# Reciprocals of the WKV recurrence in two steps of 256 columns

## The chip, the cores and the metric

The kernel runs on one core of a Trainium2 chip. The core has a matrix engine (PE), three engines for elementwise work (DVE, ACT and POOL) and SP, whose queue issues most of the transfers. Each engine takes its instructions in the order of its own queue, and semaphores hold an instruction back until what it needs is there. The metric is the device time of one execution in microseconds (us), less being better. Before the change the median of three runs is 1221.08 us (1217.28 to 1223.45).

## The reference, cut to what matters

The input x has 16 sequences of 512 tokens with 256 channels. It is normalised to `xn`; one branch is an RWKV layer (time mixing with a recurrence, then channel mixing), the other a mixture of eight experts that picks tokens by rank. The result is `x + s * silu(g)`.

```
x = _ln(x, ln0_w, ln0_b);  h = _ln(x, ln1_w, ln1_b);  xx = _time_shift(h)
xk = h * tmk + xx * (1 - tmk)          # likewise xv, xr
k = xk @ Wk.T;  v = xv @ Wv.T;  sr = sigmoid(xr @ Wr.T)
...
def step(carry, kv_t):                 # over the 512 tokens
    ww = u + kt;  p = max(pp, ww);  e1 = exp(pp - p);  e2 = exp(ww - p)
    y = (e1 * aa + e2 * vt) / (e1 * bb + e2)
...
x = x + (sr * att) @ Wo.T;  h2 = _ln(x, ln2_w, ln2_b)
kf = square(relu(xk2 @ Wfk.T));  kv = kf @ Wfv.T
s = x + sigmoid(xr2 @ Wfr.T) * kv
...
probs = softmax(xn @ Wg);  _, top_idx = top_k(probs.T, cap)   # capacity per expert
out = sum over experts e of gate_e * gelu(xn @ W1[e]) @ W2[e]
```

The division in `y` and the sigmoid of `sr` are done together: the kernel multiplies the denominator by `1 + exp(-r)` and takes one reciprocal of the product. That reciprocal is what the change touches.

## The kernel before, in words

A sequence (an "image" b, 0 to 15) is worked on with channels on the 128 partitions and the 512 tokens along the free dimension, in two halves h of 128 channels. `recurrent(b)` (L652) is a generator of nine steps for one image:

- the first normalisation `n_1` and its transposes `nps_1`, from which ACT makes `hp` (L542);
- the mixes `mix_k`, `mix_v`, `mix_r` (L549 on ACT, then L550 on DVE) and the projections k, v, r (PE, L600), copied out by ACT as `kT` (L675), `vT` (L679) and `erT` (L685);
- `wkv` for h = 0 and h = 1 (L606 to L638): a running maximum (scan L619), exponents on ACT (L625 to L628, tile `ex`), two scans (L629, L633), products (L630, L634, L636), the reciprocal (L637) and the product that puts the result back into `vT` (L638);
- the output projection `o` (PE, L643) and its addition to `x0` on DVE (L695); the second normalisation `n_2` (statistics on DVE L229 and L231, the power on POOL, the scaling on ACT L239);
- the transposes `nps_2` and the mixes `mix_k2`, `mix_r2` (L563 on ACT, then L566 on DVE, both reading `nps_2` in PSUM);
- the wide projection `f` (PE, L600, eight blocks), relu and square on ACT (L707, L708) to `kf`;
- `fr` and `kv` (PE, L643), joined on DVE by L733 and L735.

Here `ex_7_0` means the tile `ex` of image 7, half 0, and so on.

Beside it run, in steps dealt out by the list at L903 and the table `rest_of` at L928: the router's logits for all images, then `route()` (L295), a long chain of small steps that finds each expert's threshold bit by bit. One bit is a `Sign` with a sum on ACT (L343), a small matmul `total` on PE (L346) and `took` (L348) and `less` (L354) on DVE. After the bits come the selection and places (L363 to L408 and on to L503), which give the row numbers `holds` and `goes`. From then on `expert(i)` (L742) gathers 256 rows `xs` (POOL, L751), transposes them (`xsps`, PE L757; `xsT`, ACT L759), multiplies by `w1` (`h`, L768), takes the gelu (L773), multiplies by `w2` (`y`, L643), copies the result to `ys` (L780, by whichever engine the framework chooses, DVE or ACT) and scatters it (POOL, L782). Thirty-six expert blocks are always done and a few more if a count says so (L804).

After the experts, `outputs` (L872) and `soon` (L863) read back the expert results `y` (L816, L821) and the stored `s` (L878): ACT takes a tanh (L830), DVE makes the gates (L831) and products (L842), and POOL adds them to the output in DRAM (L845). The last two images are finished directly; the last one loads x again as `xl` (L867, issued at L215) and writes four pieces from SP (L855).

What sets the order: the framework records the instructions, and when the program is built it orders every engine's queue by readiness and by its own estimates of how long instructions take. Where `tc.issue_after` stands, an order is forced. Buffers are taken in rotation: the PSUM pool `pp_tr` (transposes) has two, `pp_mm` (k, v, r, f, h) three, `pp_ot` (o, fr, kv, y) two; in SBUF the tag `eact` has four (the expert activations, later the halves `y9_0`, `y14_0`, `y15_0` and so on).

Of the kernel before, what the change touches and what calls it, by code (L numbers as in the profile page):

```python
# [19 lines left out]
P = 128  # L20
# [6 lines left out]
def rwkv_times_moe_kernel(ctx: ExitStack, tc: tile.TileContext, a, out: bass.AP):  # L27
# [10 lines left out]
    nc = tc.nc  # L38
    x = a["x"]
    B, T, C = x.shape  # L40
# [104 lines left out]
    def col(name, h, of=cols):  # L145
        i = VECS.index(name) * NC + h
        return of[:, i : i + 1]
# [434 lines left out]
    def in_turn(buffers):  # L582
        buffers.append(buffers.pop(0))
        return buffers[-1]
# [21 lines left out]
    def wkv(kT, vT, erT, h, name):  # L606

        k, v, er = kT[:, h, :], vT[:, h, :], erT[:, h, :]
        w, u = wcol[:, h : h + 1], col("time_first", h)
        pp, ba = in_turn(pps), in_turn(bas)
        pp0, ba0 = pp[:, 0:T], ba[:, :, 0:T]
        nc.vector.tensor_tensor_scan(pp[:, 1:], w.to_broadcast([P, T]), k, -1e38, ALU.add, ALU.max)  # L619


        ex = work.tile([P, 5, T], F32, tag="ex", bufs=2, name=f"ex_{name}")
        nc.vector.scalar_tensor_tensor(ex[:, 3, :], pp0, w, k, ALU.add, ALU.subtract)
        nc.vector.scalar_tensor_tensor(ex[:, 4, :], k, u, pp0, ALU.add, ALU.subtract)
        nc.scalar.activation(ex[:, 0, :], ex[:, 3, :], AF.Relu)  # L625
        nc.scalar.activation(ex[:, 2, :], ex[:, 3, :], AF.Relu, scale=-1.0)
        nc.scalar.activation(ex[:, 1, :], ex[:, 4, :], AF.Relu, scale=-1.0, bias=top)
        nc.scalar.activation(ex[:, 0:3, :], ex[:, 0:3, :], AF.Exp, scale=-1.0)  # L628
        nc.vector.tensor_tensor_scan(ba[:, 0, 1:], ex[:, 2, :], ex[:, 0, :], 0.0, ALU.mult, ALU.add)  # L629
        nc.vector.tensor_tensor(  # L630
            ex[:, 3:5, :], ex[:, 0:2, :], v[:, None, :].to_broadcast([P, 2, T]), ALU.mult
        )
        nc.vector.tensor_tensor_scan(ba[:, 1, 1:], ex[:, 2, :], ex[:, 3, :], 0.0, ALU.mult, ALU.add)  # L633
        nc.vector.scalar_tensor_tensor(ba0, ba0, math.exp(-TOP), ex[:, 1:5:3, :], ALU.mult, ALU.add)  # L634
        den = ex[:, 0, :]
        nc.vector.scalar_tensor_tensor(den, er, 1.0, ba0[:, 0, :], ALU.add, ALU.mult)  # L636
        nc.vector.reciprocal(den, den)  # L637
        nc.vector.tensor_tensor(v, ba0[:, 1, :], den, ALU.mult)  # L638

    def token_major(lhsT_of, w, n, j, ps, jj):  # L640
# [11 lines left out]
    def recurrent(b, done, soon):  # L652
# [34 lines left out]
        for h in range(NC):  # L687
            wkv(kT, vT, erT, h, f"{b}_{h}")
            yield
# [299 lines left out]
```

## Time and profile before

| what | value |
|---|---|
| median of 3 runs | 1221.08 us |
| profiled execution | 1215.99 us, its span 1214.2 us |
| PE busy | 1118.9 us (92% of the span) |
| DVE busy | 782.9 us (64%) |
| ACT busy | 714.6 us (59%) |
| POOL busy | 370.6 us (31%) |
| mean granted PE clock | 0.971 |

The profiled execution is 5.1 us shorter than the median; 1.8 us of it lie outside the span. All places in time below are us from the start of the span. A line of a timeline gives the start, the length, the engine, the line of the kernel, the operation, the tiles as out<-in, the shape and the number of instructions merged into the line; behind it, in brackets, the idle time of the engine just before and what ended it. A line of a table of groups gives the group, its busy time in us with the mean of one instruction in ns, and then the engine's idle time before such instructions. PE executes one float32 matmul of the program as two, so its counts are twice the program's.

### The profile page before, as it was taken

The page shows a single profiled execution, that of the slowest core. Times are in us where ns is not written, and L with a number is a line of the kernel's source. Part 1 is how long each engine was busy: PE and PEld are TensorE (multiplying, and loading weights), DVE is VectorE, ACT ScalarE, POOL GpSimd, SP SyncE. Part 2 cuts the span into 40 slices and gives each one's busy share as a digit, 9 for nine tenths or more (in the row PEclk, how much of TensorE's full clock was granted, in tenths as well). Part 3 has the DMA queues.
Part 4 walks back from the last instruction along what each step waited for, and adds up shares of the span by engine and source line. Part 5 has one row for each costly group of instructions (what it writes and reads, how often), then busy time and mean ns, then how long its engine had stood idle before and what let it go on. Part 6 is the DMA issues. An engine that isn't in the chain of part 4 may idle for free. (4 is left out here: it accounts for less than half of the span.)

```text
span 1214.2 us, 12759 instructions
## 1 busy us (share of the span) xinstructions
PE 1118.9 (92%) x4333; PEld 770.6 (63%) x4333; DVE 782.9 (64%) x1324; ACT 714.6 (59%) x1158; POOL 370.6 (31%) x479
## 2 busy tenths in 40 slices
PE   4887989579999999999999999999999999899988
PEld 2444646345848768586675857768577685647555
DVE  6888587985572844728457183572736637699954
ACT  4775965347383753928448284582745828576832
POOL 7522020043232514216152251511424112243221
PEclk8998999698999999999999999999999999989989
DMA  7681020232323314223141331413232210878353
GB/s 244 224 295 52 1 104 1 104 112 76 90 70 104 130 61 126 66 90 113 41 139 52 107 102 35 139 57 121 66 104 87 91 65 18 229 171 180 96 104 53
DMA packets 69056, 125.14 MB, mean 103 GB/s; under 512 B 6263, under 2 KB 44173, under 8 KB 68749
## 3 DMA queue, kind: packets, MB, share of 16 engines
q1 hardware_dynamic: 53916, 97.55, 24.1%
q0 software_dynamic: 15072, 26.75, 10.1%
q8 instruction: 35, 0.57, 0.2%
q14 instruction: 33, 0.26, 0.1%
HBM read 90.72 MB, written 41.42 MB: 109 GB/s over the span
## 5 line engine op out<-in xcount | busy, mean ns | idle before, releaser
L600 PE MATMUL f<-mix_k,WfkT_sb 128*128 128x512 f32 x512 | 235.1, 614 | 13.4 <-DVE mix_k L566 13.4
L643 PE MATMUL kv<-WfvT_sb,kf 128*128 128x256 f32 x1024 | 228.8, 380 | 1.7 <-ACT frs L718 0.7
L643 PEld LDWEIGHTS kv<-WfvT_sb,kf 128*128 128x128 f32 x1024 | 193.5, 190 | 29.4 <-ACT frs L718 1.1
L782 POOL DMA_INDIRECT ys_d<-ys,goes x72 | 81.4, 1131 | 400.4 <-ACT ys L780 311.2
L600 PEld LDWEIGHTS f<-mix_k,WfkT_sb 128*128 128x128 f32 x512 | 97.2, 195 | 129.0 <-issue 99.4
L733 DVE SCALAR_TENSOR_TENSOR frs<-frs,kv 128x512 f32<-128x512 f32 x30 | 20.5, 685 | 199.8 <-PE kv L643 199.8
L643 PE MATMUL y<-w,act 128*128 128x256 f32 x576 | 133.6, 380 | 1.3 <-ACT act L773 1.3
L768 PE MATMUL h<-xsT,w 128*128 128x256 f32 x576 | 130.2, 379 | 0.0
L768 PEld LDWEIGHTS h<-xsT,w 128*128 128x128 f32 x576 | 109.4, 190 | 16.6 <-issue 1.9
L643 PEld LDWEIGHTS y<-w,act 128*128 128x128 f32 x576 | 107.1, 190 | 20.3 <-issue 5.3
L637 DVE RECIPROCAL ex<-ex 128x512 f32<-128x512 f32 x32 | 107.2, 3349 | 0.6
L751 POOL DMA_INDIRECT xs<-xn_d,holds x72 | 78.7, 1093 | 79.5 <-PE xsps L757 60.9
L707 ACT ACTIVATE kf<-f 128x512 f32<-128x512 f32 x128 | 74.4, 592 | 33.1 <-PE f L600 32.1
L718 ACT ACTIVATE frs<-fr 128x512 f32<-128x512 f32 x32 | 19.0, 595 | 110.4 <-PE fr L643 110.4
L780 ACT COPY ys<-y 128x512 f32<-128x512 f32 x32 | 18.7, 583 | 97.7 <-PE y L643 97.6
L629 DVE TENSOR_TENSOR_SCAN ba<-ex 128x512 f32<-128x512 f32 x32 | 39.0, 1218 | 56.4 <-ACT ex L628 56.4
L239 ACT ACTIVATE n<-x,nm,rs 128x256 f32<-128x256 f32 x128 | 68.5, 594 | 10.2 <-POOL nm L237 10.2
L643 PE MATMUL o<-WoT_sb,vT 128*128 128x256 f32 x256 | 64.7, 399 | 7.1 <-DVE frs L733 6.0
L708 ACT ACTIVATE kf<-kf 128x1024 f32<-128x1024 f32 x64 | 67.5, 1054 | 1.0
L600 PE MATMUL k<-mix_k,WkT_sb 128*128 128x512 f32 x128 | 62.7, 625 | 5.3 <-DVE mix_k L550 5.3
L773 ACT ACTIVATE act<-h 128x512 f32<-128x512 f32 x72 | 41.8, 597 | 41.4 <-PE h L768 41.1
L643 PE MATMUL fr<-WfrT_sb,mix_r 128*128 128x256 f32 x256 | 60.9, 380 | 1.1 <-ACTq L804 1.1
(223 smaller groups left out, 1894.6 us busy)
## 6 DMA issues: line engine op xcount, KB each, us to landing
w<-in_W_dram SPq DMA_DIRECT2D x72, 512.0 KB, 3.9
xa<-in_x_dram SPq DMA_DIRECT2D x16, 512.0 KB, 4.7
xn_d<-xn SPq DMA_DIRECT2D x16, 512.0 KB, 8.0
out_dram<-in_x_dram SPq DMA_DIRECT2D x15, 512.0 KB, 4.7
xc<-xn_d SPq DMA_DIRECT2D x14, 512.0 KB, 5.0
s_d<-x SPq DMA_DIRECT2D x14, 512.0 KB, 2.6
s<-s_d SPq DMA_DIRECT2D x14, 512.0 KB
out_dram<-s POOLq DMA_DIRECT2D x28, 256.0 KB, 5.9
```

What stands on the lines that cost most here:

```text
L239: nc.scalar.activation(dst[:, j, :], src[:, j, :], AF.Identity, bias=nm[:, j : j + 1], scale=rs[:, j : j + 1])
L600: mm = nc.tensor.matmul(ps, lhsT=w[:, h, o * P : (o + 1) * P], rhs=src[:, h, :], start=(h == 0), stop=(h == NC - 1))
L629: nc.vector.tensor_tensor_scan(ba[:, 0, 1:], ex[:, 2, :], ex[:, 0, :], 0.0, ALU.mult, ALU.add)
L637: nc.vector.reciprocal(den, den)
L643: mm = nc.tensor.matmul(ps[:, jj, :], lhsT=lhsT_of(c, j), rhs=w[:, c, :], start=(c == 0), stop=(c == n - 1))
L707: nc.scalar.activation(t[:, o, :], project(wfk, xk2, q * 2 + o, f"f_{b}_{q}_{o}"), AF.Relu)
L708: nc.scalar.activation(t, t, AF.Square)
L733: nc.vector.scalar_tensor_tensor(fr, fr, 1.0, psv, ALU.add, ALU.mult)
L751: nc.gpsimd.indirect_dma_start(out=xs[:, j, :], out_offset=None, in_=xn_d[:, :], in_offset=rows_at(holds, 2 * i + j))
L768: nc.tensor.matmul(ps[:, ff, :], lhsT=w1[:, h, (f + ff) * P : (f + ff + 1) * P], rhs=xsT[:, h, :], start=(h == 0), stop=(h == NC - 1),)
L773: nc.scalar.activation(act, ps, AF.Gelu)
L782: nc.gpsimd.indirect_dma_start(out=ys_d[:, :], out_offset=rows_at(goes, 2 * i + j), in_=y[:, j, :], in_offset=None)
```

## The change

The reciprocal of 512 columns (L637) becomes a loop over two halves of 256 columns; T is 512 and P is 128. Each of the 32 calls of `wkv` issues two reciprocals instead of one; nothing else is written differently.

```
-        nc.vector.reciprocal(den, den)
+        for t0 in range(0, T, P * 2):
+            nc.vector.reciprocal(den[:, t0 : t0 + P * 2], den[:, t0 : t0 + P * 2])
         nc.vector.tensor_tensor(v, ba0[:, 1, :], den, ALU.mult)
```

## The prediction

> **What bounds the kernel now.** I read the stretches by engine first, then PE's and DVE's timelines around each wait of PE, then the end of the chain. Between 303 and 1035 us PE is busy 719.75 of 732 us, at full clock:
>
> ```profile
> 303.00:1035.00 732.00, 719.75 (x2890) 519.57 (x2888) 409.57 (x575) 421.74 (x643) 230.68 (x268) 1.00 0.27 86
> 1062.40:1155.00 92.60, 85.71 (x275) 50.93 (x275) 89.79 (x138) 68.52 (x119) 32.77 (x33) 0.96 0.66 147
> ```
>
> (Columns: stretch, length, busy of PE, PE's weight loads, DVE, ACT, POOL, then clock and DMA.) There DVE works 56% of the time, so time is gained or lost only in PE's 12 us of waits. From 1062 to 1155 DVE is busy 89.8 of 92.6 us and bounds. What a reciprocal costs, from the groups kept apart by shape:
>
> ```profile
> L637 DVE RECIPROCAL ex<-ex 128x512 f32<-128x512 f32 x32 | 107.2, 3349 | 0.6
> L312 DVE RECIPROCAL red<-red 128x64 f32<-128x64 f32 x1 | 0.5, 518 | 0.0
> ```
>
> It is the longest DVE instruction of the stage, and what is queued behind it waits 3.35 us. Two such places, in DVE's and PE's timelines, image 6 and then image 5:
>
> ```profile
> 572.15 3.35 DVE L637 RECIPROCAL ex<-ex 128x512 f32<-128x512 f32 x1
> 575.42 1.31 DVE L566 SCALAR_TENSOR_TENSOR mix_k<-nps,cmk,mix_k 128x512 f32<-128x512 f32 x2
> ...
> 576.13 14.00 PE L600 MATMUL f<-mix_k,WfkT_sb 128*128 128x512 f32 x32 [1.98 <-DVE mix_k L566]
> ...
> 497.38 3.34 DVE L637 RECIPROCAL ex<-ex 128x512 f32<-128x512 f32 x1
> 500.64 1.31 DVE L566 SCALAR_TENSOR_TENSOR mix_r<-nps,cmr,mix_r 128x512 f32<-128x512 f32 x2
> ...
> 501.39 0.63 PE L757 MATMUL xsps<-ident,xs 128*128 128x128 f32 x4 [0.67 <-issue]
> ```
>
> In the first, PE idles 1.98 us for `mix_k2`, which stands behind a reciprocal. In the second, `xsps` takes the PSUM buffer of `nps_2`; its last reader, the first `mix_r2`, ends about 501.3, 0.1 us before PE goes on. The end of the chain, by SP, ACT and PE:
>
> ```profile
> 1158.09 0.68 DVE L733 SCALAR_TENSOR_TENSOR frs<-frs,kv 128x512 f32<-128x512 f32 x1
> 1158.83 3.72 PE L643 MATMUL o<-WoT_sb,vT 128*128 128x256 f32 x16 [1.51 <-DVE frs L733]
> 1162.86 0.39 SPq L215 DMA_DIRECT2D xl<-in_x_dram  x1
> 1163.30 12.54 SPq L821 DMA_DIRECT2D y<-ys_d  x2
> 1169.63 0.91 ACT L830 ACTIVATE th<-y,half_weight_of 128x256 f32<-128x256 f32 x2 [11.67 <-DMA y<-ys_d]
> 1170.44 2.06 ACT L239 ACTIVATE n<-x,nm,rs 128x256 f32<-128x256 f32 x4
> 1174.76 16.03 PE L600 MATMUL f<-mix_k,WfkT_sb 128*128 128x512 f32 x32 [0.88 <-DVE mix_k L566]
> ```
>
> ACT's `n_2` of the last image stands behind a tanh that waits for the load of `y15_0`. SP issued that load at 1163.30, right behind `xl`, which had waited for POOL's output of `s10` (issued 1157.27; such outputs take 5.9 us to land).
>
> **The direct cost.** Between 64 and 512 columns the slope is (3349 - 518) / 448 = 6.32 ns a column and the fixed part 114 ns, so 256 columns take 1.73 us and a pair 3.46. That is 0.11 us more for each call, 3.6 us of DVE time for 32. No 256-column reciprocal is in the trace. The bounds: 0 (the starts of independent DVE neighbours overlap by 0.08 us, which nearly pays for it) and 0.15 us (DVE's group L354 on 128x1, 0.15 us, taken as all overhead). I take the line through the two reciprocals. From 303 to 1035 it is hidden under PE (without that cover, 20 calls, 2.3 us). On the path are perhaps 5 others, in routing and after 1062: **+0.5 us** (0 to 1.8, if all 12 count).
>
> The Trainium skill ("VectorE: DVE Perf Modes", section on the TRN2 errata) says that operations from SBUF pay a fixed latency per instruction and advises tiles of 512 elements or more, with a measured fixed term near 150 cycles at 0.96 GHz. By it the 32 extra instructions would cost an estimated 5.0 us of DVE time against 3.6 by the rows, whose fixed part is 114 ns. It speaks against the change; the cover is the same for both.
>
> **What moves.** The built program's order of instructions, engine by engine, shows that the framework does more than split: shorter instructions let it place others between and after the halves.
>
> (a) Images 6 and 8: the queue becomes half, both `mix_k2`, half, both `mix_r2`, L638. The first `mix_k2` ends 3.35 - 1.73 = 1.62 us sooner, at 574.5; its ACT part ended at 572.7 and PE is free at about 574. PE also moves the last matmul of `y_14` (`y_21`) behind `f`: two of 0.22 us, 0.43 back. Net 1.62 - 0.43 = 1.2 us each (PE waits 1.98 us in both, at 576.13 and 725.66): **-2.4**. Next late: `ys14` is copied at about 589.7 instead of 577.3, so its PSUM buffer is free that late. `kv_6_0` needs it at 1.72 + 3.45 + 0.44 us after `f` and the moved matmul, 594.4: 4 us of cover. Its two scatters on POOL go from 578.2 to 589.8 and end near 593.7; the next gathers, issued at 594.3, then slip under 1 us and are used some 20 us later.
>
> (b) Images 5, 7 and 9: the queue becomes half, both `mix_r2`, half. The first `mix_r2` ends 1.6 us sooner, so the waits of `xsps` (0.67, 0.79 and 0.78 us) go: 2.2 us. Given back: ACT's order now puts the table load and L628 (1.28 + 1.48 us) ahead of the second relu of `f`, which frees a PSUM buffer at about 507.4, when PE wants it at 507.2. I take 0.2 each: **-1.6**. `ys10` and `ys17` go from ACT to DVE (0.69 us each) ahead of L638; the next DVE instruction waits for ACT until 508, which covers it.
>
> (c) The end. DVE still bounds; the sum of its work up to 1155 is the same but for 0.11 a call, and its order is other. `mix_k15` comes before one `s8` product, and two `s9` products and a gate are put behind `mix_k214`. Less stands ahead of `mix_k214`, so `f_14` starts near 1131.6 instead of 1132.96. Two `s10` products (0.80), two `y11` gates (1.20) and L638 (0.60) fall behind the L733 of image 14, and 1.4 us come before it. Counted from the scan L629 at 1135.6, which ACT still sets: 4 x 1.13 for scans and products, 1.4 for the moved ones, 0.6, 3.46, then L629, L638, L630, gate, L633, s10, L634, gate, s10, L636 (1.13 x 4 + 0.6 x 4 + 0.4 x 2 = 7.7), 3.46, 0.6 gives 1157.4 at the end of L733 (1158.8 before) and 1158.0 at that of L638. `o_15` needs the one for its PSUM buffer and the other from its second matmul on, so it runs as from 1157.6, 1.2 us earlier. SP's queue has `y15_0` ahead of `y13` and `xl`. It then waits only for its buffer, freed by the products of `y14_0` (L842). After L638 come L735, one `s10` and these two, 0.6 + 0.4 + 0.8, so they end at 1159.8: issue 1159.9, landing after 6.2 as before (1163.3 to 1169.5), 1166.1. Tanh to 1167.0, `n_2` to 1169.0. PE ends `o` and `kv` at 1157.6 + 3.45 + 6.95 = 1168.0, the transposes behind the last `n_2` at 1169.5; L563 and L566 take 0.75 each: `f_15` at 1171.0 instead of 1174.76, 3.8 less. `y13` is issued about 2.7 us later and wanted at 1186, `xl` at 1197. Next late: `y15_2`, whose tanh stands second in ACT's queue under `f_15`. Issued at 1171.9 and landing in 5.1 (median of such loads) it comes at 1177.0, and the relu of the second block behind it could hold PE; that costs 0 to 1.7. I take 0.3: **-3.5**.
>
> (d) Routing, 142 to 245 us. The halves let `less` of bits 17 and 14 pass after 1.7 instead of 3.35 us, and the bits run some 1.5 us ahead. But the scan L629 of image 2 now stands before `took` of bit 0, waits there for ACT's exp (about 189.1), and most of that recurrence, 9.2 us of DVE work, goes before and into the selection. `at_least` comes near 193.9 instead of 190.48. The same work would otherwise stand later in the same queue: adding up the queue, L408 ends near 210.4 instead of 211.93, and PE, which has `kv_1` to do, reaches the next transposes at 211.0 to 211.75 instead of 211.99. I take **-0.3**, bounds -1.5 and +9.3 (nothing given back).
>
> Sum: 0.5 - 2.4 - 1.6 - 3.5 - 0.3 = -7.3. On the profiled execution, 1215.99 to 1208.7; on the median of the runs, 5.1 higher, 1221.08 to 1213.8.
>
> **Rivals.**
>
> R1, the end gives nothing: another load or product is last in place of `y15_0`, or ACT stalls on `y15_2`. For it: DMA was busy 74% from 1155 to 1175. Against: in the new order no other load stands between the freed buffer and `y15_0`. Only the direct cost, (a), (b), (d) are left: -3.8, **1217.3**.
>
> R2, routing slower: L629 waiting for ACT in front of `took0` holds the selection, and the queue does not make it good. Price 9.3 us plus about 1.7 for one stretch of PE at half clock, against -7.3 and (d)'s 0.3: **1225**. It decides from L408 ending 8 us later than 211.93. For it: from 212 to 243 us PE is busy only 16.1 us and everything waits for DVE. Against: DVE had over 7 us of idle time between 181 and 190 us that this fills.
>
> R3, the clock: `f_15` took 16.03 us, `f_14` 14.00 after a wait of 2.46. If the shorter gap keeps `f_15` and its transposes at full clock, 2 to 3 us more are gained: **1211.3**. The Trainium skill ("TensorE: Matmul & The Clock Gate", Part 1) says that the clock halves after an idle window of about 3.4 us that runs freely, so a gap of 1.6 us would not halve it; the trace agrees at 576 us (1.98 idle, no loss) and not at 1079, where `f` took 15.70 us after 2.36 idle.
>
> R4, the split costs and the moved orders are hidden anyway: +0.5 to +1.8, **1222**. Against: two of PE's waits name the instruction behind the reciprocal.
>
> **How the numbers follow.** Forecast 0.45 (own range 1210 to 1217), R1 0.18, R3 0.19, R2 0.12, R4 0.06. Half a per cent is 6.1 us, about what a measurement of this kernel tells from no change; faster by that is below 1215. The forecast falls there in about 0.75 of its cases (0.34), R3 nearly always (0.18), R1 in a third (0.06): 0.58. R2 above 1227 and unseen losses of PSUM waits: 0.12; the rest, 0.30, is within. The range goes from R3 with noise, 1206, to R2 just short, 1223.
>
> **What would show it.** Right: 64 reciprocals near 1.73 us; PE's waits at `f` of images 6 and 8 near 0.4 us and no wait at `xsps` of 5, 7 and 9; `y15_0` issued within 0.3 us of the L842 of `y14_0`; `f_15` about 7.6 us ahead of its old place in a span near 1206.9. Wrong: L408 later than 212; PE waiting for PSUM before `kv_6_0`; ACT idle under `f_15` for `y15_2`; reciprocals well over 1.8 us.

## The result and the profile after

The changed kernel takes 1209.18 us (median of 4 runs, 1207.52 to 1211.03) against 1220.94 us of the kernel before (4 runs, 1217.28 to 1223.45). The ratio is 0.9913, with a 95% interval of 0.9892 to 0.9933: faster by 0.87%. The prediction was 1213.8 us. The profiled execution took 1209.01 us with a span of 1207.2 us, where 1206.9 was forecast. So the two profiled executions are 7.0 us apart, as predicted (7.3), and the medians 11.8. Both numbers have to be explained.

First the costliest group of the change and the stretches by engine, after (columns as before: stretch, length, busy of PE, PE's weight loads, DVE, ACT, POOL, then clock, DMA share and GB/s). The stretches are those of before, cut where the same work ends now:

```profile
L638 DVE RECIPROCAL ex<-ex 128x256 f32<-128x256 f32 x64 | 108.9, 1730 | 0.6
```

```profile
303.00:1032.20 729.20, 720.32 (x2890) 519.58 (x2888) 411.97 (x597) 420.62 (x641) 227.48 (x268) 1.00 0.27 86
1059.70:1150.70 91.00, 85.28 (x273) 50.46 (x272) 87.00 (x141) 68.34 (x119) 30.66 (x32) 0.96 0.68 152
```

PE does the same work in the long stretch (720.3 against 719.8 us) and its waits have shrunk from 12.3 to 8.9 us. DVE is no less busy there. What went is waiting. (After L637 the line numbers of the changed kernel are one higher: L638 is the reciprocal.)

The places that the prediction named, in the changed kernel's timelines of DVE and PE, image 6 and then (PE alone) image 5:

```profile
571.97 1.75 DVE L638 RECIPROCAL ex<-ex 128x256 f32<-128x256 f32 x1
573.64 1.31 DVE L566 SCALAR_TENSOR_TENSOR mix_k<-nps,cmk,mix_k 128x512 f32<-128x512 f32 x2
574.34 14.00 PE L600 MATMUL f<-mix_k,WfkT_sb 128*128 128x512 f32 x32 [0.81 <-DVE mix_k L566]
...
499.82 0.63 PE L758 MATMUL xsps<-ident,xs 128*128 128x128 f32 x4
507.63 7.13 PE L600 MATMUL f<-mix_k,WfkT_sb 128*128 128x512 f32 x16 [0.32 <-ACT kf L708]
```

In image 6 `mix_k2` stands behind half a reciprocal, and PE waits 0.81 us for it where it waited 1.98. In image 5 `xsps` no longer waits, but in the middle of `f` there is a new wait of 0.32 us, for the relu on ACT that frees a PSUM buffer.

The end, by SP, ACT and PE:

```profile
1154.49 3.88 PE L644 MATMUL o<-WoT_sb,vT 128*128 128x256 f32 x16 [1.17 <-DVE frs L734]
1156.85 0.32 SPq L822 DMA_DIRECT2D y<-ys_d  x1
1158.21 7.07 PE L644 MATMUL kv<-WfvT_sb,kf 128*128 128x256 f32 x32
1159.71 0.91 ACT L831 ACTIVATE th<-y,half_weight_of 128x256 f32<-128x256 f32 x2 [5.76 <-DVE x L696]
1163.59 2.07 ACT L239 ACTIVATE n<-x,nm,rs 128x256 f32<-128x256 f32 x4 [2.97 <-POOL nm L237]
1164.83 0.39 SPq L215 DMA_DIRECT2D xl<-in_x_dram  x1
1168.13 15.70 PE L600 MATMUL f<-mix_k,WfkT_sb 128*128 128x512 f32 x32 [1.65 <-DVE mix_k L566]
```

`y15_0` is issued at 1156.85, 8.0 us ahead of `xl`, and its tanh runs at 1159.71. The normalisation `n_2` is released by POOL's `nm`, not by the tanh. It ends at 1165.7, `kv` on PE at 1165.3, and `f_15` follows by the last transposes and one mix. It starts 6.6 us earlier than before.

Places in time against the kernel before, from PE's timelines of the two profiled executions, show where the 7.0 us come from:

| place | before | after | earlier by | gained since the last place |
|---|---|---|---|---|
| f_4 (all of routing is past) | 425.01 | 425.04 | -0.03 | 0.0 |
| o_6 (image 5 is past) | 547.18 | 547.00 | 0.18 | 0.2 |
| k_8 (image 6) | 630.22 | 628.87 | 1.35 | 1.2 |
| o_8 (image 7) | 696.71 | 695.14 | 1.57 | 0.2 |
| k_10 (image 8) | 779.75 | 777.03 | 2.72 | 1.2 |
| o_10 (image 9) | 846.25 | 843.49 | 2.76 | 0.0 |
| o_14 | 1113.68 | 1110.90 | 2.78 | 0.0 |
| o_15 | 1158.83 | 1154.49 | 4.34 | 1.6 |
| f_15 | 1174.76 | 1168.13 | 6.63 | 2.3 |
| end of the span | 1214.2 | 1207.2 | 7.0 | 0.4 |

### The profile page after: what moved, and what is told of

It reads as the page before. It is cut to its first block, busy times and chain, and to the rows that moved or that the text cites. A ratio compares the mean times of both kernels' runs of the same rounds, so it can differ in the third digit from the quotient of the medians.

```text
span 1207.2 us, 12796 instructions
## 1 busy us (share of the span) xinstructions
PE 1118.0 (93%) x4333; PEld 769.5 (64%) x4333; DVE 785.1 (65%) x1358; ACT 713.3 (59%) x1156; POOL 366.9 (30%) x479
## 5 line engine op out<-in xcount | busy, mean ns | idle before, releaser
L600 PE MATMUL f<-mix_k,WfkT_sb 128*128 128x512 f32 x512 | 236.7, 617 | 13.2 <-DVE mix_k L566 12.0
L783 POOL DMA_INDIRECT ys_d<-ys,goes x72 | 78.6, 1092 | 423.7 <-ACT ys L781 309.4
L734 DVE SCALAR_TENSOR_TENSOR frs<-frs,kv 128x512 f32<-128x512 f32 x30 | 20.5, 682 | 199.3 <-PE kv L644 199.2
L769 PEld LDWEIGHTS h<-xsT,w 128*128 128x128 f32 x576 | 109.4, 190 | 15.7 <-issue 1.0
L638 DVE RECIPROCAL ex<-ex 128x256 f32<-128x256 f32 x64 | 108.9, 1730 | 0.6
L629 DVE TENSOR_TENSOR_SCAN ba<-ex 128x512 f32<-128x512 f32 x32 | 39.0, 1220 | 54.2 <-ACT ex L628 54.2
L774 ACT ACTIVATE act<-h 128x512 f32<-128x512 f32 x72 | 42.0, 597 | 41.7 <-PE h L769 40.4
```

Source lines behind the costliest of these rows:

```text
L600: mm = nc.tensor.matmul(ps, lhsT=w[:, h, o * P : (o + 1) * P], rhs=src[:, h, :], start=(h == 0), stop=(h == NC - 1))
L638: nc.vector.reciprocal(den[:, t0 : t0 + P * 2], den[:, t0 : t0 + P * 2])
L734: nc.vector.scalar_tensor_tensor(fr, fr, 1.0, psv, ALU.add, ALU.mult)
L769: nc.tensor.matmul(ps[:, ff, :], lhsT=w1[:, h, (f + ff) * P : (f + ff + 1) * P], rhs=xsT[:, h, :], start=(h == 0), stop=(h == NC - 1),)
L774: nc.scalar.activation(act, ps, AF.Gelu)
L783: nc.gpsimd.indirect_dma_start(out=ys_d[:, :], out_offset=rows_at(goes, 2 * i + j), in_=y[:, j, :], in_offset=None)
```

## The experiments

All kernels were profiled, and timed beside the kernel before. Two theories stood against each other from the start. **A, the order**: a reciprocal costs the same in one piece or two, and the time comes from the places of a few instructions in the queues, each place by itself. **B, the length**: shorter reciprocals let everything pass sooner, or the gain of one place needs that of another. To read all traces alike, the span is cut at two starts of PE: `f_4` and `f_12`. Everything up to `f_4` is loading and routing, from there to `f_12` PE bounds, and behind `f_12` comes the end. The last column but one is the time from the first matmul of `o_15` to that of `f_15`.

| kernel | f_4 at | f_4 to f_12 | f_12 to PE's last | length of f_6, f_8 | o_15 to f_15 | ratio to before (interval) |
|---|---|---|---|---|---|---|
| before | 425.0 | 595.6 | 188.3 | 14.0, 14.0 | 15.9 | |
| before_again | 425.8 | 595.5 | 187.9 | 14.0, 14.0 | 16.6 | 1.0019 (1.0002 to 1.0036) |
| early_only | 426.5 | 595.5 | 188.7 | 14.0, 14.0 | 15.9 | 0.9972 (0.9958 to 0.9985) |
| middle_only | 423.8 | 593.1 | 187.3 | 14.0, 14.0 | 16.8 | 0.9975 (0.9963 to 0.9986) |
| behind_whole | 425.1 | 591.9 | 188.0 | see below | 16.4 | 0.9961 (0.9946 to 0.9975) |
| late_only | 425.7 | 598.9 | 182.6 | 15.7, 15.7 | 13.3 | 0.9948 (0.9932 to 0.9965) |
| y15_first | 427.0 | 597.6 | 183.5 | 15.7, 14.0 | 13.1 | 0.9968 (0.9953 to 0.9983) |
| after | 425.0 | 592.8 | 184.1 | 14.0, 14.0 | 13.6 | 0.9913 (0.9892 to 0.9933) |
| after_again | 420.8 | 592.8 | 183.8 | 14.0, 14.0 | 13.7 | 0.9902 (0.9877 to 0.9927) |
| after_relu | 425.1 | 592.5 | 184.9 | 14.0, 14.0 | 13.7 | 0.9898 (0.9870 to 0.9926) |
| quarters | 425.6 | 592.9 | 181.9 | see below | 13.2 | 0.9911 (0.9890 to 0.9932) |
| combined | 427.5 | 590.9 | 183.5 | see below | 13.3 | 0.9902 (0.9878 to 0.9926) |
| xl_first | 421.8 | 592.9 | 193.5 | 14.0, 14.0 | 18.6 | 0.9976 (0.9962 to 0.9991) |
| gates_first | 426.8 | 590.9 | 198.9 | see below | 15.5 | 1.0027 (1.0013 to 1.0041) |

("See below": PE puts some matmuls of `y` between those of `f`, or waits inside it.) The unchanged kernel before_again came out at 1.0019, with an interval that leaves out 1, so a difference of 0.2 or 0.3% between two ratios says little. The second column varies by over 6 us over the traces (420.8 to 427.5) and by 4 even in one kernel (425.0 and 420.8 in the changed one); one trace says little about it. For what happens behind `f_4` the third and fourth columns carry the verdicts.

### The change in one part of the images

`early_only`, `middle_only` and `late_only` divide the reciprocals of some images only; the order of the queues elsewhere is then that of before. The edits are to the kernel before.

```
-        nc.vector.reciprocal(den, den)
+        for t0, n in ((0, P * 2), (P * 2, P * 2)) if <image> else ((0, T),):
+            nc.vector.reciprocal(den[:, t0 : t0 + n], den[:, t0 : t0 + n])
```

with `<image>` an image number below 5, from 5 to 9, or above 13.

> Two steps in images 14 and 15 alone, one piece elsewhere; the order behind 1062 us is then that of the changed kernel and the order ahead of it that of before. If the end's own order gives the end's gain (theory A), every place up to the o of image 14 stands where it stood in the trace of before (1113.68 us, within 0.2), and from there to the end 4.2 us are gained: f_15 near 1170.9, a span near 1210.0 against 1214.2 of before. If the end's gain needs the time gained further up (rival B, buffers and transfers meeting earlier work), less than 2 us are gained. The medians of before and after differ by 11.7 us and their traces by 7.0, so 4 to 5 us are still without a place: if they lie at the end, the ratio is near 0.993 (8 to 9 us), if elsewhere, near 0.9965 (4.2 us).

> Two steps in images 5 to 9 alone. Theory A: f_6 starts 1.8 us earlier than in the trace of before (574.3), f_8 3.2 earlier (722.5), f_12 2.8 earlier (1017.8), the same as in the changed kernel, and nothing is added behind: a span 2.8 us shorter, 1211.4, ratio 0.998. Rival B (the gain of the middle is lost at the end, where another wait ends last, unless the end is reordered too): f_13 is 2.8 us earlier, but the end less than 1 us. If the 4 to 5 us without a place lie here, the ratio is near 0.994.

> Two steps in images 0 to 4 alone, which is the routing stretch and what follows it up to f_4. In the first pair of traces this part moved f_4 by 0.03 us. Theory A: the ratio is 1.000 and f_4 stands where the kernel before has it, between 424 and 428 us in its own traces and in those of the kernels that differ from it only later. Rival G (the routing's new order gains on average what one pair of traces does not show: f_4 of the three traces with the new order stands 1.4 us earlier than in the first trace of before on average, of the seven with the old order 0.7 later): f_4 near 423.6 and a ratio near 0.998.

**Measured.** early_only gains nothing in its trace (f_4 to f_12 595.5, the end 188.7) and f_4 is not early (426.5), which speaks against rival G. But its ratio of 0.9972, with an interval below 1, is the one that rival G had set, and one trace does not settle where `f_4` stands on average. By the ratios the early part (0.28%) weighs as much as the middle (0.25%), with 0.52% for the end; the three add up to 1.05%, the whole change to 0.87 and 0.98%. So rival G stays open, and is taken up in after_again. middle_only gains 2.5 us by `f_12`, as the changed kernel does (2.8), and keeps them to the end. late_only has the whole of the end's gain without any gain in the middle: o_15 to f_15 takes 13.3 us, and DVE's shorter path from f_13 to o_15 gives another 1.6 us once f_14's length is allowed for (79.6 us with an f_14 of 15.70, against 79.5 with 14.00 before). **What follows.** The middle and the end are independent, as theory A has it. But the sums of late_only are disturbed by something new: the stretch from f_4 to f_12 is 3.3 us longer than in before, with the same instructions. PE's timeline of late_only shows the place, and the record of the granted clock beside it, in two windows of 3.41 us (columns as before):

```profile
576.82 15.70 PE L600 MATMUL f<-mix_k,WfkT_sb 128*128 128x512 f32 x32 [1.98 <-DVE mix_k L566]
```

```profile
574.81:578.22 3.41, 1.43 (x5) 0.68 (x5) 3.41 (x5) 3.40 (x4) 0.00 (x0) 1.00 0.60 192
578.22:581.63 3.41, 3.41 (x6) 1.34 (x5) 3.41 (x5) 1.02 (x2) 1.66 (x1) 0.50 0.11 38
```

and the same in before, whose wait there is as long:

```profile
574.72:578.13 3.41, 2.00 (x5) 1.04 (x6) 3.41 (x6) 3.24 (x4) 0.00 (x0) 1.00 0.53 161
578.13:581.54 3.41, 3.41 (x9) 1.50 (x9) 3.38 (x5) 2.24 (x3) 1.66 (x1) 1.00 0.11 38
```

In late_only PE works at half clock for 3.41 us of `f`, which then takes 15.70 us in place of 14.00. The trace of before has the same wait and no such loss. This is taken up in before_again, and what tells the two apart in the last section.

### One whole reciprocal, put behind the mixes

The kernel before, with no reciprocal divided; in images 5, 7 and 9 the next image's reciprocal is forced behind both `mix_r2`, in 6 and 8 behind both `mix_k2`:

```
-        nc.vector.reciprocal(den, den)
+        with tc.issue_after(mixed_at[behind[name]].ins) if name in behind else nullcontext(): nc.vector.reciprocal(den, den)
```

(`mixed_at` keeps the last L566 of each mix.)

> No reciprocal is divided. In images 5, 7 and 9 the reciprocal of the next image is put behind both mix_r2, in images 6 and 8 behind both mix_k2, by the forced order alone. If only the place of the reciprocal in DVE's queue counts (theory A), the whole reciprocals give the middle what the halves gave: f_6 about 1.0 us earlier than its place in image 5 would have it, f_8 the same again, no wait at xsps of 5, 7 and 9, 2 to 3 us by f_12. If the shorter instruction itself is what helps (rival B: a reciprocal of 3.35 us in any place holds something that PE waits for), f_12 gains less than 1 us and a new wait of PE of 1 us or more shows within 15 us behind the moved reciprocals. The end is that of before, so the ratio is near 0.998 under A and 1.000 under B.

**Measured.** DVE's and PE's timelines of behind_whole at image 6:

```profile
571.89 1.46 DVE L566 SCALAR_TENSOR_TENSOR mix_k<-nps,cmk,mix_k 128x512 f32<-128x512 f32 x2
573.55 0.75 DVE L566 SCALAR_TENSOR_TENSOR mix_r<-nps,cmr,mix_r 128x512 f32<-128x512 f32 x1 [0.19 <-ACT mix_r L563]
574.22 3.34 DVE L637 RECIPROCAL ex<-ex 128x512 f32<-128x512 f32 x1
572.69 5.42 PE L600 MATMUL f<-mix_k,WfkT_sb 128*128 128x512 f32 x12 [0.41 <-DVE mix_k L566]
```

`f_6` starts at 572.69 with 0.41 us of wait; PE does the rest of `y_14` between and behind its blocks. By `f_12` 3.7 us are gained, 1.55 each in images 6 and 8 and 0.2 each in 5, 7 and 9. **What follows.** The whole reciprocal in a better place gives more than the halves (2.8 us), and no new wait of 1 us showed behind the moved reciprocals. Rival B falls: the gain of the middle needs no shorter instruction. What counts is how much stands ahead of the mixes in DVE's queue. The halves let the framework's planner take half a reciprocal out of their way in images 6 and 8; moving the whole takes all of it.

### Four steps

```
-        nc.vector.reciprocal(den, den)
+        for t0 in range(0, T, P):
+            nc.vector.reciprocal(den[:, t0 : t0 + P], den[:, t0 : t0 + P])
```

> Four steps of 128 columns everywhere. By the line through 3349 ns at 512 and 1730 ns at 256 columns (6.32 ns a column and 112 ns) one takes 0.92 us; since the pair of 256 took 3.36 us from start to end, 0.02 more than the one piece, four in a row take 3.4 to 3.5 us. Theory A (place in the queue counts, not length): in images 6 and 8 the first mix_k2 is 0.8 us earlier, but the second stands behind two quarters and is ready when it was, so f gains no more than 0.3 us; middle and end as in the changed kernel within 1 us, ratio 0.990 to 0.993. Rival B (shorter is better throughout): another 2 us or more are gained. Rival H (96 more instructions than before cost DVE their fixed part at the end, where it bounds): the stretch from k_14 to the last o is 0.5 to 1 us longer.

**Measured.** The group of the reciprocals by shape in quarters:

```profile
L638 DVE RECIPROCAL ex<-ex 128x128 f32<-128x128 f32 x128 | 110.6, 915 | 0.6
```

915 ns each, but where four stand in a row DVE's timeline has them in 3.38 to 3.39 us from the first start to the last end; two halves in a row, as in 21 of the 32 calls of the changed kernel, take 3.35 to 3.37 and the whole 3.34 to 3.35. The means add up to more (4 x 0.915 = 3.66) because each starts before the one ahead has ended. The middle takes 592.9 us, as with two steps. The end is 2.3 us shorter than in the changed kernel, of which 1.7 is `f_15` at 14.00 in place of 15.70 us; the rest, 0.6 us in one trace, has no test. The path that rival H names, from k_14 to the last o, takes 40.2 against 40.1 us. **What follows.** By the medians dividing costs 0.01 us for two in a row and 0.03 us for four, next to nothing even where DVE bounds; rival H falls with it, and B again: twice as fine does not gain another 2 us, and the ratio is that of two steps.

### The load of y15_0

`y15_first` is the kernel before with one transfer moved: `xl` is forced behind the load of `y15_0`.

```
-            at_last.append(load(x, b, "xl", tag="x"))
+            with tc.issue_after(y15[-2].ins): at_last.append(load(x, b, "xl", tag="x"))
```

`xl_first` is the changed kernel with the opposite order forced; the planner then puts the tanh of `y15_0` behind `n_2` on ACT.

> The kernel before with one transfer moved: the load of y15_0 stands ahead of xl in SP's queue; DVE's two last instructions of the same stretch change places and nothing else does. My prediction had 2.4 of the 3.5 us at the end come from this load. Theory A1 (the load is what n_2 waits for through the tanh): y15_0 is issued about 1161.0 instead of 1163.3, the tanh runs at 1166 or sooner instead of 1169.6, n_2 goes when its statistics are there, and f_15 starts 1.5 to 2 us earlier, near 1173, bounded by kv ending at 1169.4. Rival A2 (DVE's products, not the load, set it): f_15 is within 0.5 us of 1174.76 because the load lands late all the same. Ratio 0.9985 under A1, 1.000 under A2.

> The changed kernel with the load of y15_0 put back behind xl in SP's queue; the tanh of y15_0 then stands behind n_2 of the last image in ACT's queue, and nothing else changes. Theory A3 (what held n_2 was that the tanh stands ahead of it in ACT's queue, so a late load is harmless behind it): n_2 starts as soon as its statistics are there, f_15 starts 9.5 to 10 us behind the last o as in the changed kernel (1168.13 after 1158.37, its first matmul at 1154.49), and the end is the same within 1 us; y15_0 lands under f_15. Rival A4 (the load itself matters, because its late landing delays DVE's products and the relus under f_15): PE waits for a relu inside f_15 or for PSUM in fr, and the end is 2 us or more later. Ratio 0.990 to 0.993 under A3, 0.9935 under A4.

**Measured.** SP, ACT and PE of y15_first (this execution stands some 4 us later than that of before when it reaches the end):

```profile
1165.04 0.32 SPq L821 DMA_DIRECT2D y<-ys_d  x1
1165.97 0.39 SPq L215 DMA_DIRECT2D xl<-in_x_dram  x1
1168.08 0.91 ACT L830 ACTIVATE th<-y,half_weight_of 128x256 f32<-128x256 f32 x2 [6.07 <-DMA y<-ys_d]
1171.77 2.07 ACT L239 ACTIVATE n<-x,nm,rs 128x256 f32<-128x256 f32 x4 [2.78 <-POOL nm L237]
1175.96 14.00 PE L600 MATMUL f<-mix_k,WfkT_sb 128*128 128x512 f32 x32 [1.29 <-DVE mix_k L566]
```

and of xl_first:

```profile
1164.10 0.39 SPq L215 DMA_DIRECT2D xl<-in_x_dram  x1
1164.54 9.91 SPq L822 DMA_DIRECT2D y<-ys_d  x2
1163.91 2.08 ACT L239 ACTIVATE n<-x,nm,rs 128x256 f32<-128x256 f32 x4 [9.63 <-POOL nm L237]
1169.70 0.91 ACT L831 ACTIVATE th<-y,half_weight_of 128x256 f32<-128x256 f32 x2 [3.71 <-DMA y<-ys_d]
1173.38 16.65 PE L600 MATMUL f<-mix_k,WfkT_sb 128*128 128x512 f32 x32 [6.57 <-DVE mix_k L566]
```

With the one load moved, `f_15` starts 13.1 us behind `o_15` in place of 15.9, and takes 14.00 us in place of 16.03: 4.8 us in all behind `f_12`. Ahead of `xl`, `y15_0` released its tanh 3.0 us after its issue (1165.04 to 1168.08); right behind `xl` this took 6.3 in before (1163.30 to 1169.63) and 5.2 in xl_first (1164.54 to 1169.70). In xl_first `n_2` does go without the tanh, but the tanh is still ahead of L563, and that of the mixes: the wait only moved by one instruction on ACT, and PE waits 6.57 us. **What follows.** A1 holds, with a larger effect than expected (2.9 against 1.5 to 2 us): the load comes sooner because it is issued sooner, 2.2 us behind the start of `o_15` in place of 4.5, and because it takes half as long. That the second is `xl` standing ahead of it in the queue is the likely reading; no run changed that alone. A3 falls in the form in which I wrote it, and A4's two places (relu, `fr`) were not it either: what counts is that no instruction on ACT ahead of the mixes waits for a late load.

### The wait that took the place of xsps

The changed kernel, with the exponents of the next image forced behind the second relu of `f` in images 5, 7 and 9:

```
-        nc.scalar.activation(ex[:, 0:3, :], ex[:, 0:3, :], AF.Exp, scale=-1.0)
+        with tc.issue_after(relu_at[relu_first[name]].ins) if name in relu_first else nullcontext(): nc.scalar.activation(ex[:, 0:3, :], ex[:, 0:3, :], AF.Exp, scale=-1.0)
```

> The changed kernel with one forced order: in images 5, 7 and 9 the exponents L628 of the next image's second half come behind the second relu of f, so that this PSUM buffer of f is read before ACT's table load and exponents. My prediction's step (b) expected 1.6 us from images 5, 7 and 9 and the trace gave 0.5. Theory E (the freed wait went into PE's next wait, for ACT's relu): the waits of 0.32, 0.32 and 0.51 us inside f of these images go, the stretch from f_4 to f_5 and o_7 is 0.3 to 0.5 us shorter for each of the three, together 1.0 to 1.4 us by f_12. Rival F (the 0.67 to 0.79 us of the xsps waits were never PE time that could be had, because matmuls ahead of them were still running): the relu waits go and less than 0.3 us is gained in all, or the wait moves to the next block of f. Ratio to the changed kernel 0.999, to before 0.9915 to 0.994.

**Measured.** PE's timeline of image 5 in after_relu: `f` has no wait inside any more.

```profile
500.39 14.21 PE L600 MATMUL f<-mix_k,WfkT_sb 128*128 128x512 f32 x32
```

Images 5 and 7 gain 0.5 us each against before (0.2 in the changed kernel); image 9 gains nothing, since PE's wait of 0.52 us there is for a later relu. Image 8 gives 0.3 us back: PE's wait there for the gelu (L774), ahead of `f_8`, is 0.58 us in place of 0.26. By `f_12` 0.24 us are left of the 1.0 to 1.4 expected. **What follows.** The cause that theory E names is shown in two of three images: part of what was freed at `xsps` had gone into the next wait in the same `f`. But the sum is rival F's, less than 0.3 us, because half of the gain went into a further wait. The ratio does not tell so little apart.

### The kernel before, once more, and the changed one

> The kernel before once more, for a second trace of it. Theory C (the clock): PE's wait of 1.98 us ahead of f_6 and of f_8 halves the granted clock in some executions and not in others; two of the four such waits in the runs late_only and y15_first were followed by an f of 15.70 us in place of 14.00 in both images or one, none in the first trace of before. Then f_6 and f_8 are each 14.00 or 15.70 here and nothing between, the rest of 303 to 1035 is the same within 0.3 us, and the span is 1214 to 1218. Rival D (the other executions of before are longer because of loads and routing ahead of 303 us, not of the clock): f_6 and f_8 take 14.00 again and what differs lies ahead of 303 us. Ratio 1.000.

> The changed kernel once more, on the chip of this call. Theory C: its waits of 0.81 us ahead of f_6 and f_8 never halve the clock, so both f take 14.00; f_13 to f_15 can each be 14.0 or 15.6 to 16.0. Ratio between 0.992 and 0.995: 7.0 us of the traces, and 1.7 us for about half of two waits of before, 8.7 of 1219. Under rival D the ratio is 0.9943, the traces' 7.0 us alone.

(Counted rightly, three of the four waits named there were followed by an `f` of 15.70 us, not two.) **Measured.** The second trace of before has 14.00 us at both places, like the first. Over the five traces with the old order there, before, before_again, early_only, late_only and y15_first, three of ten waits of 1.98 us were followed by an `f` of 15.70 us, seven by 14.00, none by anything between. In the nine with a new order the waits are 0.41 to 0.88 us, and none of eighteen lost clock. At 1.7 us each this is 1.0 us of an average execution of before, which no single trace shows as such (the ten waits are few; the last section says which of them lost clock). Theory C is right in kind, but too small for the whole: the changed kernel's ratio here is 0.9902, 11.7 us by the means of the runs on this chip (1206.2 over 4, 1217.9 over 13).

Every run has its mean granted clock. Within one kernel time falls with it: over 20 executions of before on one chip by 0.48 us for each 0.001 (correlation -0.71), on two others by 0.73 and 0.62 (13 and 29 executions, -0.82 and -0.76). The 13 of this chip have a mean of 0.970 and the changed kernel 0.976; the first traces of the two, which are 7.0 us apart, have 0.971 and 0.973. The means are thus 0.004 further apart than the traces, and at about 0.6 us for 0.001 that is an estimated 2.4 us of the 4.7 that the traces leave over. It is an argument from a correlation, and the other 2.3 us have no place.

Part of them may lie ahead of `f_4`, where rival G of early_only looks. From `f_1` to `f_2`, in routing, PE takes 99.2 to 100.4 us in all eight traces whose reciprocals are whole there (images 0 to 4) and in four of the six where they are divided, but 96.0 in after_again and 96.9 in xl_first, which both have only 20.5 us at half clock between 210 and 300 us (23.9 to 30.7 in the other twelve). `f_4` stands at 425.8 on average in the eight and at 424.1 in the six. With six and eight traces that scatter by 4 to 6 us this proves nothing; it fits early_only's ratio.

### All together, and one step further

`combined` is the kernel before with the placed whole reciprocals of behind_whole, the relus of after_relu, and halves in images 14 and 15 alone. `gates_first` adds one forced order: the products of `s2` go behind L735 of image 12.

```
-            nc.vector.scalar_tensor_tensor(
+            with tc.issue_after(frs_at[12, 2].ins) if b == 2 else nullcontext(): nc.vector.scalar_tensor_tensor(
                 half[:, jj, :], gate[:, jj, :], half_of(b, j0 + jj), half[:, jj, :], ALU.mult, ALU.mult
             )
```

(`frs_at` keeps the L735 of each image.)

> Whole reciprocals placed by forced order in images 5 to 9 as in behind_whole, the relu order of after_relu, and the two steps only in images 14 and 15 as in late_only. If the three are independent (theory A: each place has its own wait), they add: 3.7 us of behind_whole, 1.2 of the relus, 4.2 of the end, 9.1 us against the trace of before and 2 less than the changed kernel: ratio 0.991 to 0.9925, 0.998 of after_again. If they share a wait (rival B), the sum is no more than the changed kernel's 7 us.

> The kernel combined, with the products of s2 put behind L735 of image 12's second half. In all traces so far DVE stands 6.2 us in front of these products for the load of s2, and PE waits 4.4 to 4.7 us ahead of the second half of o in image 13 for the L733 queued behind them. Theory A (a queue's head that waits for a transfer holds what PE needs): the wait of 4.4 us goes, f_13 starts 2 to 4 us earlier by its distance from f_12 (58.7 us so far), and the whole is 2 us or more faster than combined. Rival B (the transfers bound that stretch, DMA is busy 0.93 to 0.96 of it): another product or gate waits for its load in turn, and less than 1 us is gained by the end.

**Measured.** combined has, with gates_first, the shortest middle, 590.9 us, 1.9 less than the changed kernel, and the end of late_only (o_15 to f_15 13.3 us). The gains add up in the trace: 4.7 and 4.8 us against before, with an `f_14` of 15.70 us in it. Its median is 1206.97 us on the chip where the changed kernel has 1206.28, ratio 0.9902 for both. So no version beats the changed kernel measurably. Behind `f_4` combined's trace is 2.3 us shorter than after_again's (774.4 against 776.7) and yet its median is not; its reciprocals in routing are whole, so this too fits rival G.

gates_first is 15 us slower than combined in PE's last instruction counted from f_12. DVE and PE, at image 13:

```profile
1082.51 0.48 DVE L844 SCALAR_TENSOR_TENSOR s<-y,half_weight_of,s 128x256 f32<-128x256 f32 x1 [4.90 <-DMA s<-s_d]
1083.57 1.39 DVE L566 SCALAR_TENSOR_TENSOR mix_k<-nps,cmk,mix_k 128x512 f32<-128x512 f32 x2
1084.36 16.05 PE L600 MATMUL f<-mix_k,WfkT_sb 128*128 128x512 f32 x32 [7.78 <-DVE mix_k L566]
```

**What follows.** The wait of `o_13` shrank from 4.7 to 3.2 us. The products put back are done by 1061.5; the one at 1082.51 is the thirteenth in DVE's queue from there, and so of the third image behind `s2`. In combined it stands behind the mixes of image 13 (1085.17), here ahead of them, and waits for its own load. So the forced order made the planner move something else too, in front of what `f_13` needs. It came as rival B has it, another product waiting for its load in turn; that the loads bound the stretch is not shown beyond that.

## Why the prediction was right

**The direct cost** (+0.5, bounds 0 and 1.8) was mis-sized. The fixed part of 114 ns that the line gives is real, each half has 1730 ns, but it overlaps the neighbour: two in a row end 0.01 us later than the whole, by the medians (3.365 and 3.353). The lower bound, which I had written beside it with this very overlap as its reason, was right, and the measured cost is next to nothing. The rule of the Trainium skill that spoke against the change ("VectorE: DVE Perf Modes", section on the TRN2 errata) would have had 5.0 us of DVE time; the busy sum rose by 1.7 us (108.9 against 107.2), and nearly all of that stands in the 11 calls whose halves have something else between them. For independent neighbours in one queue the measurement decides against it.

**(a)**, images 6 and 8, -2.4: measured 1.17 and 1.15, together -2.3. The mechanism and the size were right, with the moved matmul of `y_14` paid for as worked out. `kv_6_0` did not wait for PSUM: `ys14` was copied by 589.5, and `kv_6_0` started at 594.23. What the step lacked is the clock: the wait of 1.98 us cost 1.7 us more in 3 of 10 cases, and the one trace that I had happened to show none. That the size fits the two traces so well is in part the luck of that.

**(b)**, images 5, 7 and 9, -1.6: measured 0.22, 0.22 and 0.04, together -0.5. The `xsps` waits went as said. The step that failed is "given back, I take 0.2 each": what was given back is 0.45, 0.57 and 0.74 (the old wait less the gain), and the waits for relus that PE's timeline shows are 0.32, 0.32 and 0.51 of it; the rest, 0.13 to 0.25, has no line of its own. The relu was named as the next late thing, and after_relu confirms it in images 5 and 7, but it was priced as if the ends worked out by hand (507.4 against 507.2) were good to a tenth.

**(c)**, the end, -3.5: measured -4.2. `o_15` came 1.6 us earlier than its lead at `o_14` (1.2 forecast), `f_15` 3.85 us (3.8 forecast), and `f_15` itself took 0.3 us less. The load of `y15_0` was the carrier, shown from both sides by y15_first and xl_first. One number on the way was wrong: I gave the load its old 6.2 us, and it took under 3, with `xl` no longer just ahead of it. So `n_2` waited for POOL's `nm` and not for the tanh, which the working did not have. It did not matter, because `kv` on PE ended as late as `n_2` did (1165.3 and 1165.7), close to where the working had put both. The feared wait for `y15_2` cost nothing that PE shows.

**(d)**, routing, -0.3: measured 0.0 at `f_4` in this pair of traces (after_again has more to say on it). The way there was wrong. In DVE's timeline of the changed kernel:

```profile
190.66 1.23 DVE L629 TENSOR_TENSOR_SCAN ba<-ex 128x512 f32<-128x512 f32 x1 [0.78 <-ACT ex L628]
195.44 0.14 DVE L363 TENSOR_SCALAR at_least<-less 128x1 f32<-128x1 f32 x1
212.16 0.69 DVE L408 TENSOR_TENSOR route_w<-route_w,first 128x512 f32<-128x512 f32 x1
```

L629 does stand there waiting for ACT (0.78 us), but the bits were not 1.5 us ahead, `at_least` came at 195.44 and not 193.9, and L408 ended at 212.85, later than the 212 that I had set as the sign of an error. Still nothing reached `f_2` (0.05 us): R2's mechanism was there with 0.9 us, of the 8 at which it would have decided, and what follows made it good. (The 16.1 us of PE work that R2 names between 212 and 243 us are 16.8 in the trace, which changes nothing.)

**R3**, the clock at `f_15`, did not come in the changed kernel: 15.70 us, not 14.00. It did come in late_only, y15_first, quarters and combined, where `f_15` took 14.00 behind a wait of 1.29 to 1.30 us; in after, after_again and after_relu, behind 1.64 to 1.65, it took 15.7 (and 17.05 in gates_first, behind 1.30). So the sentence that a gap of 1.6 us would not halve the clock does not hold here. The measured median is nearer to R3's 1211.3 than to the forecast, but not for R3's reason. R1 and R4 are excluded by the trace.

**The median.** The sum for the traces was 0.3 us off, partly by luck: (b) promised 1.1 us too much, and the direct cost and (c) were 0.5 and 0.7 too cautious. Yet the median came 4.6 us below the forecast. What failed is the sentence "on the median of the runs, 5.1 higher": I carried the distance between before's profiled execution and its median over to the changed kernel, whose profiled execution is 0.2 us below its median. That distance is not a constant. It belongs to what a kernel loses in some executions and not in others, and a wait of PE that disappears takes its part of it along: counted for the two waits of 1.98 us (about 1 us), argued from the clock for about 1.4 more, open for the rest. The median lies just below the range that the forecast itself was given, 1210 to 1217; the whole range, 1206 to 1223, was wide enough.

## What to carry to other kernels

Where a scheduler fills the queues, the length of an instruction is also an input to its order: read what else moved before pricing the edit, and test the order by itself with the old instruction in the new place. In front of an engine that bounds, look for what its next input is queued behind, on every engine of the way back, transfers included; when one such wait goes, find the next in the same block and price it from a trace, not by subtracting two times worked out by hand. And one profiled execution shows a lucky or an unlucky throw of whatever varies: compare several before carrying its distance to the median over. Where the trace has a record of the clock, look at how PE's waits lie in its windows, and not only at how long they are.

## What the hardware showed beyond that

A wait of PE of 1.98 us halved its clock in three of ten cases and cost then 1.70 us of a 14.00 us block; waits of 0.41 to 0.88 us in the same place never did (0 of 18); one of 2.36 us and more ahead of `f_13` always did (14 of 14, 15.49 us and more). Length alone doesn't decide: ahead of `f_14` a wait of 2.46 us lost nothing in six of six traces, one of 2.66 us something in four of seven.

What decides can be read from the 14 traces. Their records of the granted clock hold two values, 1 and 0.5, and within one trace every change lies on a grid of 3.413 us. From 281 us on, 51 windows of this grid at full clock had 1.97 us or more in which PE was idle, and the next window was at half clock behind all 51. Behind the 3671 windows with less than 1.6 us it was at half clock never, and behind the 18 between in eight; in each of these eight, transposes were part of what PE did. So it counts how much of a wait falls into one window. Of the ten waits of 1.98 us three lay wholly in one, as in the lines of late_only, and these are the three that lost clock; the other seven were cut by a border, which left 1.22 to 1.96 us in one window, as the 1.41 in the lines of before. A wait of 0.41 to 0.88 us can't reach 1.97 by itself. Ahead of `f_15` the transposes' small waits add to it: 1.75 to 1.77 us in a window where `f_15` took 15.7 us in the changed kernel, 1.30 to 1.41 where it took 14.00. In before, where it took 16.03 behind a wait of only 0.88 us, 1.94 us are idle in the window ahead. From half clock PE came back behind every window with 0.52 us or less of idle time (45), and behind none with 0.66 or more (19).

The Trainium skill ("TensorE: Matmul & The Clock Gate", Part 1) says that the clock is granted by a window of about 3.4 us that runs freely, so that what happens depends on where in it the work falls, and that there are only two rates. The grid of 3.413 us, the two values and the loss of 1.70 us in one throw, half of 3.41, agree; that only idle windows of about 3.4 us throttle does not, for 1.98 us of idle time did it here.

A load of 256 KB (`y15_0`) was there 3.0 us after its issue in y15_first, ahead of the 512 KB of `xl` in the same queue, and 5.2 and 6.3 us after it right behind `xl` (xl_first and before).
